# Router logits from the output projection, two token tiles a step in two PSUM banks, and one row scatter a place

## The chip, the cores and the metric

The kernel runs on one core of one Trainium2 chip, in float32. The metric is device microseconds of a whole run, the median of three runs. One further execution was recorded by the hardware profiler; every number with a line of the code beside it comes from that one.

## The reference

The input is x (4096 tokens x 256 features) and a 4096 x 4096 matrix adj. Two layers follow each other.

```python
x = x + gnn(layernorm(x), adj, neigh_W, lin_W)   # z = [f, adj @ (f @ Wn.T) / deg] @ Wl.T
x = x + ffn(layernorm(x)[None], ...)             # below; here x stands for layernorm(x)
h = rmsnorm(x, ln1)
q, k, v = heads of h @ wq.T, wk.T, wv.T          # 4 heads, 2 key/value heads, 64 wide; q, k rotated
y = softmax(causal(q @ k.T / 8)) @ v
x = x + y @ wo.T
flat = rmsnorm(x, ln2)
probs = softmax(flat @ router_w.T)               # 8 experts
tp, ti = top_k(probs, 2)                         # weights: tp / (sum + 1e-9)
out = sum over e of weight[e] * (silu(flat @ w1[e].T) * (flat @ w3[e].T)) @ w2[e].T
return x + out
```

What matters here is the stretch from y to the two chosen experts. The router's logits are a product of the normalized sum `x + y @ wo.T`. They are linear in y before the normalization, so they can be had as `y @ (wo.T @ router.T)` plus a part from x alone, and scaled afterwards.

## The kernel before, in words

The tokens are cut into 8 blocks of 512 (`NB`), each of 4 tiles of 128 (`TB`). The program has a fixed order on each engine, written out by hand; instructions of an engine run in that order, and semaphores hold them for their data.

*Stages.* (1) The graph layer, with queries, keys and values of blocks 0 to 6 made on the way (0 to 545 us). (2) Attention, blocks in the order 3, 0, 4, 1, 5, 2, 6, 7 (545 to 1072 us). (3) The experts: groups of token rows, collected by expert in the DRAM tensor `lists`, go through w1, w3 and w2 (from 1072 us).

*Attention.* A block has two head pairs; for each, a loop goes over its key tiles. One turn of it is called a unit here. A unit makes scores five units ahead (`scores`, L738: 8 matmul passes in 64x64 tiles), has ScalarE (ACT) exponentiate them (L746), adds them to running sums on VectorE (DVE, `totals`, L764), masks diagonals on GpSimd (POOL, L748) and multiplies by V (`values`, L778) into two PSUM banks. The three banks `y_first`, `y_second`, `y_third` are taken in turn, two by each pair; the pair that ends is unloaded by ACT (L786) and then DVE (L787), so one of the three is not in use by the current pair. Scores take two more double banks, and `p_ms` is a single bank for everything else.

*Places.* All other work of a block is a list of steps, and `at` (L1522) puts each list into places; a place comes after every second unit, and there are 144. A step that works on PE takes a free place; a list entry that begins with `None` doesn't ask whether the place is free. `after(b)` (L1026) is the list that follows a block's attention: `inputs` (layernormed rows), `project` twice (L850: two token tiles x two halves of y, into one `p_ms` bank, added into `row` by DVE at L859), `logits` (L888), `squared` (ACT, then a power on POOL), `residual` (L861: POOL adds, SP stores), `weigh` (L904), `choose`, `scaled`, `place` (the row's slots in the lists) and eight `scatter`s (L1004), which are indirect DMAs issued by POOL. The normalization's inverse comes before it through DRAM: `denominators`, `inverted` (SP's DMAs, L827 and L833) and `normalize` (DVE, L840).

*Logits before.* `router_wo` folds the router into wo (`router_sb`, 32 columns of which 8 are used). `logits` multiplies it with y into four 128x32 tiles (`lgT`), ACT copies that (L901), and `weigh` transposes it (`lg`, L907) and adds the part from x (`first_lg`).

*The last block.* Its queries are not ready when attention begins. `last_qkv` (L1049) makes them in the first places: `turned` (two transposes steps, `tr_l`), and four times `rotate` (`pq_l`) and `turn_heads` (`trq_l`), one token tile a step, each in `p_ms`. Its own `after` list runs among the experts: `step` (L1588) takes one entry of `rest` at fixed points of `hidden` and after `combine`.

Of the kernel before, what the change touches and what calls it, by code (L numbers as in the profile page):

```python
# [9 lines left out]
F32 = mybir.dt.float32  # L10
# [7 lines left out]
P = 128  # L18
N = 4096
C = 256  # L20
# [46 lines left out]
def fast_kernel(  # L67
# [53 lines left out]
    for e in range(NE):  # L121
        nc.gpsimd.memset(experts[:, :, e : e + 1], float(e))
    wo_sb = const.tile([P, 2, C], F32, name="wo_sb")

# [3 lines left out]
    wqkv_sb = const.tile([P, 2, 512 + NE], F32, name="wqkv_sb")  # L128
    router_sb = const.tile([P, 2, 32], F32, name="router_sb")
    nc.gpsimd.memset(router_sb, 0.0)  # L130

# [111 lines left out]
    with (  # L243
# [49 lines left out]
        def load_rest():  # L293

            w = wqkv.rearrange("(c p) o -> p c o", p=P)
            nc.sync.dma_start(wqkv_sb[:, :, 0:QK], w[:, :, 0:QK])
            nc.sync.dma_start(wqkv_sb[:, :, QK + NE :], w[:, :, QK:])
            nc.sync.dma_start(ln1_sb, ln1)
            nc.sync.dma_start(ln2_sb, ln2)

            wo_h = wo_t.rearrange("(j p d) o -> j d p o", j=2, p=2)
            for j in range(2):
                nc.sync.dma_start(wo_sb[j * HD : (j + 1) * HD], wo_h[j])
# [24 lines left out]
        def router_wo():  # L328
            transposed_wo = qT[5][:, :, 0:C]
            ps = p_pj.tile([P, 512], F32, tag="pj", name="p_wo")  # L330
            for j in range(2):
# [5 lines left out]
            nc.scalar.copy(  # L337
                router_sb[:, :, 0:NE], ps[:, 0 : 2 * NE].rearrange("p (j e) -> p j e", j=2)
            )
# [326 lines left out]
    with (  # L666
# [37 lines left out]
        def give_back(keys):  # L704
# [4 lines left out]
        p_sa = cycle((p_sc0, p_sc2))  # L709
        y_banks = cycle([  # L710
            pool.tile([P, 512], F32, tag=tag, name=name) for pool, tag, name in (
                (p_sc1, "sc", "y_first"), (p_sc1, "sc", "y_second"), (p_y, "y", "y_third"),
            )
        ])
        HP = P // 2
# [13 lines left out]
        def scores(b, p, s):  # L729
# [17 lines left out]
            if sb == b:  # L747
# [3 lines left out]
                )  # L751
            probs[b, p, s] = pt

        def totals(b, p, s):
# [13 lines left out]
        def values(b, p, s):  # L768
# [3 lines left out]
            if s == 0:  # L772
                accs[b, p] = next(y_banks), next(y_banks)
            for k in range(2):
# [74 lines left out]

        def project(b, h):  # L850
            x2 = flats[b][:, 2 * h : 2 * h + 2, 0:C]
            ps = p_ms.tile([P, 2, C], F32, tag="ms", name=f"po_{b}_{h}")
            for t in range(2):
                for c in range(2):
                    nc.tensor.matmul(  # L855
                        ps[:, t, :], ys[b, c][:, (2 * h + t) * P : (2 * h + t + 1) * P],
                        wo_sb[:, c, :], start=(c == 0), stop=(c == 1),
                    )
            nc.vector.tensor_add(x2, x2, ps)  # L859

# [26 lines left out]

        def logits(b):  # L888


            ps = p_ms.tile([P, P], F32, tag="ms", name=f"lgT_{b}")
            for c in range(2):
                for t in range(TB):
                    nc.tensor.matmul(
                        ps[32 * t : 32 * (t + 1), :], router_sb[:, c, :],
                        ys[b, c][:, t * P : (t + 1) * P],
                        start=(c == 0), stop=(c == 1), skip_group_check=True,
                        tile_position=(0, 32 * t),
                    )
            lgT = ax.tile([P, P], F32, tag="lgT", name=f"lgs_{b}", bufs=1)  # L900
            nc.scalar.copy(lgT, ps)  # L901
            picks[b] = lgT

        def weigh(b):  # L904
            ri, lgT = squares.pop(b), picks[b]
            lg = p_ms.tile([P, TB, 32], F32, tag="ms", name=f"lg_{b}")
            nc.tensor.transpose(lg.rearrange("p t e -> p (t e)"), lgT, ident)  # L907
            pr = small("r_p", b)
            nc.vector.tensor_add(pr, lg[:, :, 0:NE], first_lg[b])
# [94 lines left out]
        def scatter(b, t, k):  # L1004
            nc.gpsimd.memset(gap, 0.0)
            put = nc.gpsimd.indirect_dma_start(  # L1006
# [19 lines left out]
        def after(b):  # L1026

            return [
                [None, lambda: inputs(b)],
                [None],  # L1030
                [lambda: project(b, 0)],
                [lambda: project(b, 1)],
                [lambda: logits(b), lambda: squared(b, 0)],
                [None, lambda: squared(b, 1), lambda: residual(b)],
                [lambda: weigh(b)],
                [None],
                [None, lambda: choose(b)],
                [None, lambda: scaled(b, 0)],
                [None, lambda: scaled(b, 1)],
                [lambda: place(b), lambda: scaled(b, 2)],  # L1040
                [None, lambda: scaled(b, 3), lambda: scatter(b, 0, 0)],
                [None, lambda: scatter(b, 0, 1), lambda: scatter(b, 1, 0)],
                [None, lambda: scatter(b, 1, 1), lambda: scatter(b, 2, 0)],
                [None, lambda: scatter(b, 2, 1), lambda: scatter(b, 3, 0)],
                [None, lambda: scatter(b, 3, 1)],
            ]


        def last_qkv():  # L1049
# [15 lines left out]

            def turned(h):
                tr = p_ms.tile([P, 2, 2, P], F32, tag="ms", name=f"tr_l{h}")
                for t in range(2):
# [8 lines left out]

            def rotate(t):
                pj = p_ms.tile([P, 512], F32, tag="ms", name=f"pq_l{t}")
                room = hTs[t % 2]  # L1080
# [10 lines left out]

            def turn_heads(t):
                tr = p_ms.tile([P, 2, 2, P], F32, tag="ms", name=f"trq_l{t}")
                heads(ax, b, t, made["hT"], *made.pop(t), tr)
                if t == TB - 1:
                    for n in range(3):
                        lend(n, "late", 1)

            return [
                [None, scales], [None, norm], [lambda: turned(0)], [lambda: turned(1)],  # L1100
                [lambda: rotate(0)], [lambda: rotate(1)],
                [lambda: turn_heads(0)], [lambda: rotate(2)],
                [lambda: turn_heads(1)], [lambda: rotate(3)],
                [lambda: turn_heads(2)], [lambda: turn_heads(3)],
                *guard(),
# [413 lines left out]
        PLACES = len(keys) // 2  # L1519
        later, taken = {}, set()  # L1520

# [30 lines left out]
        for b in ORDER[:-1]:  # L1552
            end = at(max(ends[b] + 3, end - 4), after(b))
        at(end, [[None, begin_experts]])
# [12 lines left out]
        for n, (b, p, s) in enumerate(keys):  # L1567
# [13 lines left out]


        rest = [[lambda: normalize_pair(ORDER[-1], 1)]] + after(ORDER[-1]) + [
            [lambda: make_table(NB, True, NA, NW - NA)], [lambda: make_table(NB, False, NW, NG - NW)],
        ]
        rest = iter([fs for fs in ([f for f in fs if f] for fs in rest) if fs])
# [771 lines left out]
```

## Time and profile before

| what | us |
|---|---|
| runs: lowest, median, highest | 1585.32, 1586.35, 1587.05 |
| the profiled execution, whole | 1588.64 |
| its span, first to last instruction | 1586.9 |
| of which TensorE (PE) busy | 1565.8 |
| DVE, ACT, POOL busy | 1044.6, 488.4, 600.5 |
| attention, 545 to 1072: PE, DVE, ACT, POOL busy | 519.6, 413.4, 293.6, 181.4 |
| first part of the experts, 1072 to 1140: PE, DVE busy | 68.0, 27.7 |
| rest of the experts, 1140 to 1580: PE busy, of 440 | 438.5 |

The granted clock of TensorE has a mean of 0.996. In the profile, PE is TensorE's matmuls and PEld its weight loads. A float32 matmul of the program shows as two, so `po` of a step has eight lines where the code has four calls. A row of the timeline gives the start in us, the duration, the engine, the line, the operation with the tile that it writes and those that it reads, their sizes, a count of merged rows, and in brackets how long the engine stood idle before it and what ended that. The ends of matmuls are modelled; their starts are not, so times of a step are best taken from start to start.

### The profile page before, as it was taken

The page shows a single profiled execution, that of the slowest core. Times are in us where ns is not written, and L with a number is a line of the kernel's source. Part 1 is how long each engine was busy: PE and PEld are TensorE (multiplying, and loading weights), DVE is VectorE, ACT ScalarE, POOL GpSimd, SP SyncE. Part 2 cuts the span into 40 slices and gives each one's busy share as a digit, 9 for nine tenths or more (in the row PEclk, how much of TensorE's full clock was granted, in tenths as well). Part 3 has the DMA queues.
Part 4 walks back from the last instruction along what each step waited for, and adds up shares of the span by engine and source line. Part 5 has one row for each costly group of instructions (what it writes and reads, how often), then busy time and mean ns, then how long its engine had stood idle before and what let it go on. Part 6 is the DMA issues. An engine that isn't in the chain of part 4 may idle for free.

```text
span 1586.9 us, 27471 instructions
## 1 busy us (share of the span) xinstructions
PE 1565.8 (99%) x10744; PEld 1122.2 (71%) x10744; DVE 1044.6 (66%) x2090; ACT 488.4 (31%) x892; POOL 600.5 (38%) x726
## 2 busy tenths in 40 slices
PE   8999999999999999999999999999999999999997
PEld 7888888888888543344333333338899999999996
DVE  7966676677767676978887776893565444443562
ACT  1101010010010455565555545653122222222221
POOL 3446556457456341543443420412422212122213
PEclk9999999999999999999999999999999999999999
DMA  6343434443443001111111100069767777787762
GB/s 232 127 136 133 149 126 157 136 136 133 139 137 133 4 1 29 38 36 52 41 42 32 39 29 15 32 188 352 212 186 211 252 238 238 246 262 246 262 200 29
DMA packets 72602, 213.68 MB, mean 135 GB/s; under 512 B 17488, under 2 KB 49616, under 8 KB 58832
## 3 DMA queue, kind: packets, MB, share of 16 engines
q1 hardware_dynamic: 59200, 193.84, 36.0%
q0 software_dynamic: 12720, 17.47, 5.7%
q8 instruction: 86, 1.41, 0.4%
q10 hardware_dynamic: 544, 0.52, 0.1%
q14 instruction: 52, 0.43, 0.1%
HBM read 184.48 MB, written 31.47 MB: 136 GB/s over the span
## 4 chain that ended last, share of the span: by engine, by line
PE 95%; DVE 2%; ACT 1%; another core or an unknown queue 1%; DMA 1%; issue 0%; POOL 0%; SPq 0%; POOLq 0%; DVEq 0%; ACTq 0%
PE acc L496 24%; PE h L1417 20%; PE sc L738 14%; PE y_first L778 5%; PE y_second L778 5%; PE ye_y L1469 4%; PE y_third L778 4%; PE ye_y L1381 3%; PE ye_ms L1381 2%; PE pq L197 2%; PE po L855 2%; PE ph L548 2%; PE pf L467 1%; PE tx L1318 1%; PE trq L232 1%; PE tr L379 1%
## 5 line engine op out<-in xcount | busy, mean ns | idle before, releaser
L738 PE MATMUL sc<-qT_all,kT 64*64 64x512 f32 (+3 forms) x2304 | 283.1, 563 | 5.0 <-ACT res_all L746 2.0
L496 PE MATMUL acc<-a,g 128*128 128x256 f32 x1024 | 245.9, 380 | 0.0
L496 PEld LDWEIGHTS acc<-a,g 128*128 128x128 f32 x1024 | 193.0, 190 | 31.6 <-DVE vv L514 1.2
L1489 POOL DMA_INDIRECT acc_dram<-y,late x57 | 89.8, 1576 | 305.9 <-DVE y L1484 159.5
L1424 DVE TENSOR_TENSOR late<-si,h 128x256 f32<-128x256 f32 (+2 forms) x126 | 62.7, 506 | 184.2 <-ACT si L1423 179.2
L738 PEld LDWEIGHTS sc<-qT_all,kT 64*64 64x64 f32 x2304 | 80.4, 133 | 143.2 <-issue 112.1
L746 ACT ACTIVATE pt_all<-sc 128x1024 f32<-128x1024 f32 (+3 forms) x154 | 147.8, 968 | 104.8 <-PE sc L738 94.8
L1417 PE MATMUL h<-late,qT_all 128*128 128x256 f32 (+1 forms) x792 | 147.3, 345 | 0.0
L451 POOL TENSOR_TENSOR all_s<-all_s,more_sums 128x512 f32<-128x512 f32 x72 | 105.6, 1480 | 107.2 <-DVE more_sums L443 107.2
L1423 ACT ACTIVATE si<-h 128x256 f32<-128x256 f32 (+2 forms) x126 | 57.0, 453 | 278.0 <-PE h L1417 274.2
L1417 PEld LDWEIGHTS h<-late,qT_all 128*128 128x128 f32 x792 | 130.0, 191 | 14.7 <-issue 1.0
L496 PE MATMUL acc<-more_sums,g 128*128 128x256 f32 x512 | 126.3, 379 | 0.0
L764 DVE TENSOR_TENSOR late<-late,pt_all 128x1024 f32<-128x1024 f32 (+3 forms) x87 | 104.1, 1197 | 23.8 <-ACT pt_all L746 11.3
L1417 PE MATMUL h<-late,pt_all 128*128 128x128 f32 (+1 forms) x704 | 113.5, 321 | 0.0
L1417 PEld LDWEIGHTS h<-late,pt_all 128*128 128x128 f32 x704 | 103.5, 191 | 8.0
L778 PE MATMUL y_second<-pt_all,vv 64*64 64x512 f32 (+3 forms) x448 | 108.7, 559 | 0.0
L496 PEld LDWEIGHTS acc<-more_sums,g 128*128 128x128 f32 x512 | 97.2, 190 | 14.8
L778 PE MATMUL y_first<-pt_all,vv 64*64 64x512 f32 (+2 forms) x432 | 105.2, 563 | 0.4 <-issue 0.4
L1006 POOL DMA_INDIRECT lists<-row,slots x64 | 68.4, 1069 | 69.2 <-issue 69.1
L778 PE MATMUL y_third<-pt_all,vv 64*64 64x512 f32 (+3 forms) x352 | 87.1, 572 | 0.0
L381 ACT COPY qT_all<-tr 128x512 f32<-128x512 f32 x30 | 16.2, 589 | 210.5 <-PE tr L379 210.4
L1417 PE MATMUL h<-late,res_all 128*128 128x256 f32 (+1 forms) x352 | 68.3, 353 | 0.0
(349 smaller groups left out, 2982.2 us busy)
## 6 DMA issues: line engine op xcount, KB each, us to landing
a<-in_adj_dram SPq DMA_DIRECT2D x64, 1024.0 KB
qT_all<-in_w_dram SPq DMA_DIRECT2D x18, 1408.0 KB
pt_all<-in_w_dram SPq DMA_DIRECT2D x16, 1408.0 KB
res_all<-in_w_dram SPq DMA_DIRECT2D x17, 768.0 KB
pt_all<-in_w_dram SPq DMA_DIRECT2D x16, 768.0 KB
res_all<-in_w_dram SPq DMA_DIRECT2D x8, 1408.0 KB
qT_all<-in_w_dram SPq DMA_DIRECT2D x9, 768.0 KB
late<-lists SPq DMA_DIRECT2D x25, 265.0 KB
```

The costliest lines, as they stand in the source:

```text
L451: nc.gpsimd.tensor_add(all_s[:, i], all_s[:, i], sums_at[n % 2][k])
L496: nc.tensor.matmul(acc[bank][:, at, :], g[jb][:, right, k, :], m[left][:, k, :], start=(jb == 0 and k == 0 and at == 0), stop=(jb == NB - ...
L738: nc.tensor.matmul(ps[k * HP : (k + 1) * HP, j, :w], kT[sb][hd, i * P + k * HP : i * P + (k + 1) * HP], qT[b][hd, p, off:], start=True, st ...
L746: nc.scalar.activation(pt[:, :, :w], ps[:, :, :w], AF.Exp, scale=HD ** -0.5)
L764: nc.vector.tensor_add(sums[b, p][:, :, off:], before[:, :, off:], pt[:, :, : 512 - off])
L778: nc.tensor.matmul(accs[b, p][k][hd, off:], vv[sb][some, i, hd], pt[some, j, : 512 - off], start=(s == 0), stop=(s == TB * b + TB - 1),)
L1006: put = nc.gpsimd.indirect_dma_start(out=lists[:, :], out_offset=bass.IndirectOffsetOnAxis(ap=chosen[b][:, k, t, :], axis=0), in_=flats[b] ...
L1381: nc.tensor.matmul(p[number], m[left][:, j, :], m[right][:, j, :], start=(n % 4 == 0 and j == 0), stop=(j == 2), skip_group_check=True,)
L1417: nc.tensor.matmul(ps[m % 2][:, m // 2 - q, :], w13_sb[:, c, m * P : (m + 1) * P], xT[:, c, :], start=(c == 0), stop=(c == 1),)
L1424: nc.vector.tensor_mul(hT[:, q : q + both, :], si[:, 0:both, :], ps[1][:, 0:both, :])
L1469: nc.tensor.matmul(ps[h if last else 0][:, h, :], hT[:, q, cols], w2_sb[:, q, :], start=(q == 0), stop=(q == NF),)
L1489: put = nc.gpsimd.indirect_dma_start(out=(acc_dram if k < NM - LAST else out)[:, :], out_offset=at, in_=y[:, h, :], in_offset=None, comput ...
```

## The change

- `wo_sb` gets 8 more columns, which hold the folded router (`router_sb` is gone). A projection's matmul is 264 columns wide, and its last 8 are the logits' part from y. DVE adds each tile's 256 columns into `row` and its 8 columns to `first_lg`. `logits`, its ACT copy and the transpose in `weigh` are gone.
- A step works on two token tiles in two banks: `p_ms`, and the one of the three y banks that the current pair doesn't use. This holds for the projections and for `turned`, `rotate` and `turn_heads` of the last block's queries. Places at a pair's end (`taken`) are kept free of such steps.
- The first projection of a list comes one place later, `weigh` two entries after `squared` instead of one.
- For all blocks but the last, a scatter is preceded by a copy of one column of the newest exponentials (`latest`) into `gap`, where a memset was, and there is one scatter a place, at eight places (for block 6, two at four places).
- The last block has a list of its own, `after_last`: the second normalization shares a step with `inputs`, and the four projections go one tile a step in `p_ms`.

```diff
-    wo_sb = const.tile([P, 2, C], F32, name="wo_sb")
+    wo_sb = const.tile([P, 2, C + NE], F32, name="wo_sb")
...
-        y_banks = cycle([
+        y_banks = [
...
+        def two_banks(name):
+
+            return (
+                p_ms.tile([P, 512], F32, tag="ms", name=name), y_banks[y_next[0] % 3],
+            )
...
             probs[b, p, s] = pt
+            latest[:] = [pt]
...
-        def project(b, h):
-            x2 = flats[b][:, 2 * h : 2 * h + 2, 0:C]
-            ps = p_ms.tile([P, 2, C], F32, tag="ms", name=f"po_{b}_{h}")
-            for t in range(2):
+        def project(b, tiles, rooms):
+            if tiles[0] == 0:
+                picks[b] = small("r_p", b)
+            for t, ps in zip(tiles, rooms):
                 for c in range(2):
                     nc.tensor.matmul(
-                        ps[:, t, :], ys[b, c][:, (2 * h + t) * P : (2 * h + t + 1) * P],
-                        wo_sb[:, c, :], start=(c == 0), stop=(c == 1),
-                    )
-            nc.vector.tensor_add(x2, x2, ps)
+                        ps[:, 0 : C + NE], ys[b, c][:, t * P : (t + 1) * P], wo_sb[:, c, :],
+                        start=(c == 0), stop=(c == 1),
+                    )
+            for t, ps in zip(tiles, rooms):
+                x2 = flats[b][:, t, 0:C]
+                nc.vector.tensor_add(x2, x2, ps[:, 0:C])
+                nc.vector.tensor_add(picks[b][:, t, :], ps[:, C : C + NE], first_lg[b][:, t, :])
+
+        def project_two(b, h):
+            project(b, (2 * h, 2 * h + 1), two_banks(f"po_{b}_{h}"))
+
+        def project_one(b, t):
+            project(b, (t,), (p_ms.tile([P, 512], F32, tag="ms", name=f"po_{b}_{t}"),))
...
-        def logits(b):
...
         def scatter(b, t, k):
-            nc.gpsimd.memset(gap, 0.0)
+            if b == ORDER[-1]:
+                nc.gpsimd.memset(gap, 0.0)
+            else:
+                nc.gpsimd.tensor_copy(gap, latest[0][:, 0, 0:1])
...
+            at_once = 2 if b == ORDER[-2] else 1
             return [
                 [None, lambda: inputs(b)],
                 [None],
-                [lambda: project(b, 0)],
-                [lambda: project(b, 1)],
-                [lambda: logits(b), lambda: squared(b, 0)],
+                [None],
+                [lambda: project_two(b, 0)],
+                [lambda: project_two(b, 1), lambda: squared(b, 0)],
                 [None, lambda: squared(b, 1), lambda: residual(b)],
-                [lambda: weigh(b)],
                 [None],
+                [None, lambda: weigh(b)],
...
-                [None, lambda: scaled(b, 3), lambda: scatter(b, 0, 0)],
-                [None, lambda: scatter(b, 0, 1), lambda: scatter(b, 1, 0)],
...
+                [None, lambda: scaled(b, 3)],
+                *(
+                    [None, *(lambda n=n: scatter(b, n // 2, n % 2) for n in range(n, n + at_once))]
+                    for n in range(0, 2 * TB, at_once)
+                ),
+            ]
+
+        def after_last(b):
+
+            return [
+                [lambda: normalize_pair(b, 1), lambda: inputs(b)],
+                [lambda: project_one(b, 0)],
+                [lambda: project_one(b, 1)],
+                [lambda: project_one(b, 2), lambda: squared(b, 0)],
+                [lambda: project_one(b, 3)],
+                [lambda: squared(b, 1), lambda: residual(b)],
+                [lambda: weigh(b)],
...
             return [
-                [None, scales], [None, norm], [lambda: turned(0)], [lambda: turned(1)],
-                [lambda: rotate(0)], [lambda: rotate(1)],
-                [lambda: turn_heads(0)], [lambda: rotate(2)],
-                [lambda: turn_heads(1)], [lambda: rotate(3)],
-                [lambda: turn_heads(2)], [lambda: turn_heads(3)],
+                [None, scales], [None, norm],
+                [lambda: both_of(turned, "tr", 0)], [None],
+                [lambda: both_of(rotate, "pq", 0)], [None], [None],
+                [lambda: both_of(turn_heads, "trq", 0)],
+                [lambda: both_of(rotate, "pq", 1)], [None], [None],
+                [lambda: both_of(turn_heads, "trq", 1)],
                 *guard(),
             ]
...
-        later, taken = {}, set()
+        later = {}
+        taken = {n // 2 for n, (b, p, s) in enumerate(keys) if s == TB * b + TB - 1}
...
-            end = at(max(ends[b] + 3, end - 4), after(b))
+            end = at(max(ends[b] + 3, end - 8), after(b))
...
-        rest = [[lambda: normalize_pair(ORDER[-1], 1)]] + after(ORDER[-1]) + [
-            [lambda: make_table(NB, True, NA, NW - NA)], [lambda: make_table(NB, False, NW, NG - NW)],
-        ]
+        rest = after_last(ORDER[-1])
```

More of the change, by code (lines that the diff above doesn't have):

```diff
@@ L122, in fast_kernel @@
         nc.gpsimd.memset(experts[:, :, e : e + 1], float(e))
-    wo_sb = const.tile([P, 2, C], F32, name="wo_sb")
+    wo_sb = const.tile([P, 2, C + NE], F32, name="wo_sb")
     QK = 384
     wqkv_sb = const.tile([P, 2, 512 + NE], F32, name="wqkv_sb")
-    router_sb = const.tile([P, 2, 32], F32, name="router_sb")
-    nc.gpsimd.memset(router_sb, 0.0)
     cos_l = const.tile([P, TB, HD // 2], F32, name="cos_l")
@@ L302, in load_rest @@
             for j in range(2):
-                nc.sync.dma_start(wo_sb[j * HD : (j + 1) * HD], wo_h[j])
+                nc.sync.dma_start(wo_sb[j * HD : (j + 1) * HD, :, 0:C], wo_h[j])
             nc.sync.dma_start(
@@ L337, in router_wo @@
             nc.scalar.copy(
-                router_sb[:, :, 0:NE], ps[:, 0 : 2 * NE].rearrange("p (j e) -> p j e", j=2)
+                wo_sb[:, :, C:], ps[:, 0 : 2 * NE].rearrange("p (j e) -> p j e", j=2)
             )
@@ L713, in fast_kernel, with next_bank @@
             )
-        ])
+        ]
+        y_next = [0]
+        def next_bank():
+            y_next[0] += 1
+            return y_banks[(y_next[0] - 1) % 3]
+        def two_banks(name):
+            return (
+                p_ms.tile([P, 512], F32, tag="ms", name=name), y_banks[y_next[0] % 3],
+            )
+        latest = []
         HP = P // 2
@@ L772, in values @@
             if s == 0:
-                accs[b, p] = next(y_banks), next(y_banks)
+                accs[b, p] = next_bank(), next_bank()
             for k in range(2):
@@ L886, in over @@
             return v.to_broadcast([P, TB, NE])
-        def logits(b):
[L891 to L898, printed above, removed]
-                    )
-            lgT = ax.tile([P, P], F32, tag="lgT", name=f"lgs_{b}", bufs=1)
-            nc.scalar.copy(lgT, ps)
-            picks[b] = lgT
-        def weigh(b):
[L905 to L909, printed above, removed]
+        def weigh(b):
+            ri, pr = squares.pop(b), picks[b]
             nc.vector.tensor_mul(pr, pr, over(ri))
@@ L1040, in after @@
                 [lambda: place(b), lambda: scaled(b, 2)],
-                [None, lambda: scaled(b, 3), lambda: scatter(b, 0, 0)],
-                [None, lambda: scatter(b, 0, 1), lambda: scatter(b, 1, 0)],
-                [None, lambda: scatter(b, 1, 1), lambda: scatter(b, 2, 0)],
-                [None, lambda: scatter(b, 2, 1), lambda: scatter(b, 3, 0)],
-                [None, lambda: scatter(b, 3, 1)],
+                [None, lambda: scaled(b, 3)],
[3 more added lines that the diff above has]
+                ),
+            ]
+        def after_last(b):
[7 more added lines that the diff above has]
+                [lambda: weigh(b)],
+                [lambda: choose(b)],
+                [lambda: scaled(b, 0)],
+                [lambda: scaled(b, 1)],
+                [lambda: place(b), lambda: scaled(b, 2)],
+                [lambda: scaled(b, 3), lambda: scatter(b, 0, 0)],
+                [lambda: scatter(b, 0, 1), lambda: scatter(b, 1, 0)],
+                [lambda: scatter(b, 1, 1), lambda: scatter(b, 2, 0)],
+                [lambda: scatter(b, 2, 1), lambda: scatter(b, 3, 0)],
+                [lambda: scatter(b, 3, 1)],
+                [lambda: make_table(NB, True, NA, NW - NA)],
+                [lambda: make_table(NB, False, NW, NG - NW)],
             ]
@@ L1064, in norm, with turned @@
                 made["hT"] = qT[b]
-            def turned(h):
-                tr = p_ms.tile([P, 2, 2, P], F32, tag="ms", name=f"tr_l{h}")
+            def turned(h, bank):
+                tr = bank.rearrange("p (c t i) -> p c t i", c=2, t=2)
                 for t in range(2):
@@ L1076, in turned, with rotate @@
                 )
-            def rotate(t):
-                pj = p_ms.tile([P, 512], F32, tag="ms", name=f"pq_l{t}")
+            def rotate(t, pj):
                 room = hTs[t % 2]
@@ L1090, in rotate, with turn_heads @@
                 )
-            def turn_heads(t):
-                tr = p_ms.tile([P, 2, 2, P], F32, tag="ms", name=f"trq_l{t}")
+            def turn_heads(t, bank):
+                tr = bank.rearrange("p (c t i) -> p c t i", c=2, t=2)
                 heads(ax, b, t, made["hT"], *made.pop(t), tr)
@@ L1097, in turn_heads, with both_of @@
                         lend(n, "late", 1)
+            def both_of(f, name, h):
+                for k, bank in enumerate(two_banks(f"{name}_l{h}")):
+                    f(2 * h + k, bank)
             return [
-                [None, scales], [None, norm], [lambda: turned(0)], [lambda: turned(1)],
-                [lambda: rotate(0)], [lambda: rotate(1)],
-                [lambda: turn_heads(0)], [lambda: rotate(2)],
-                [lambda: turn_heads(1)], [lambda: rotate(3)],
-                [lambda: turn_heads(2)], [lambda: turn_heads(3)],
+                [None, scales], [None, norm],
[4 more added lines that the diff above has]
+                [lambda: both_of(turn_heads, "trq", 1)],
                 *guard(),
```

## The prediction

> **What bounds the kernel now.** I read the page first, then the timeline of TensorE (PE) around the removed steps, then the list of waits.
>
> ```profile
> PE 1565.8 (99%) x10744; PEld 1122.2 (71%) x10744; DVE 1044.6 (66%) x2090; ACT 488.4 (31%) x892; POOL 600.5 (38%) x726
> ...
> PE 95%; DVE 2%; ACT 1%; another core or an unknown queue 1%; DMA 1%; issue 0%; POOL 0%; SPq 0%; POOLq 0%; DVEq 0%; ACTq 0%
> ```
>
> PE is busy for 99% and holds 95% of the chain that ended last. So I count the time of each PE step, from the start of what stands before it to the start of what comes after. In attention (545 to 1072 us) the scores (`sc`) and products with V (`y_...`) run in rounds of four 64x64 tiles. A round of 512 columns starts 0.43 us after the last: 0.833 ns a column. The next view shows what an inserted step costs.
>
> ```profile
> 621.22 0.59 PE L778 MATMUL y_first<-late,vv 64*64 64x512 f32 x1
> 621.74 1.99 PE L855 MATMUL po<-wo_sb,yT 128*128 128x256 f32 x8
> 623.67 1.09 PE L738 MATMUL sc<-qT_all,kT 64*64 64x512 f32 x8
> ...
> 632.26 0.59 PE L778 MATMUL y_first<-pt_all,vv 64*64 64x512 f32 x1
> 632.78 0.64 PE L894 MATMUL lgT<-yT,router_sb 128*32 128x128 f32 x16
> 633.35 1.09 PE L738 MATMUL sc<-qT_all,kT 64*64 64x512 f32 x8
> ...
> 639.86 0.59 PE L778 MATMUL y_first<-pt_all,vv 64*64 64x512 f32 x1
> 640.38 0.33 PE L907 MATMUL lg<-ident,lgs 128*128 128x128 f32 x1
> 640.64 0.88 PE L738 MATMUL sc<-qT_all,kT 64*64 64x384 f32 x8
> ```
>
> Without the step, `sc` would start 0.43 us after the first line of each three. So `po` takes 623.67 - 621.65 = 2.02 us, of which 8 x 256 x 0.833 ns = 1.71 is streaming: 0.31 us goes to the change of shape, whatever is in the step. `lgT` takes 0.67 and `lg` 0.35. The score's first values also start 0.91 instead of 0.86 us after it, so each insertion costs 0.05 more.
>
> PE also stands still in four spots of attention. I add up each round's start less the start before it and its streaming.
>
> ```profile
> 828.48 0.70 PE L855 MATMUL po<-wo_sb,yT 128*128 128x256 f32 x2 [1.27 <-DVE yT L840]
> ...
> 878.51 0.96 POOL L1006 DMA_INDIRECT lists<-row,slots  x1 [0.19 <-issue]
> 879.48 0.11 POOL L1005 MEMSET gap<- 128x1 f32 x1
> 879.78 0.96 POOL L1006 DMA_INDIRECT lists<-row,slots  x1 [0.19 <-issue]
> ...
> 882.25 1.94 ACT L746 ACTIVATE late<-sc 128x1024 f32<-128x1024 f32 x2 [5.48 <-remote]
> ...
> 934.22 1.02 ACT L746 ACTIVATE res_all<-sc 128x1024 f32<-128x1024 f32 x1 [4.75 <-remote]
> 935.30 1.98 PE L738 MATMUL sc<-qT_all,kT 64*64 64x512 f32 x8 [1.98 <-ACT res_all L746]
> ```
>
> At 828 `po` waits for its normalized input: 2.07 us with the second half of that wait. The others come at the end of a run of row scatters: POOL issues eight of them 1.27 us apart (870.5 to 880.7, and 922.5 to 933), since only the queue's order holds them. At the end of both runs ACT has a score to exponentiate, starts it over 4 us late, and PE stops behind it. Costs: 1.55 us at 879 to 883; 2.67 at 932 to 935, and then 2.6 more, since six rounds after it start 0.85 apart, at half the clock; 0.43 at 722. Together 7.25. Why ACT waits ("remote") the trace does not say; other runs of eight (763 to 774, 1023 to 1034) have no such stop.
>
> **What the Trainium skill says.** "TensorEngine Tiling (Array Packing)", Key Properties: "Changing tiling mode (not just tile) drains the TensorE". The 0.31 us around each 128x128 step agree. "VectorE: DVE Perf Modes", The TRN2 errata, gives (N+151)/0.96 ns for an f32 two-input add: 691 for N = 512, and the trace has 680 to 690 for L859; so I estimate 424 for 256 columns (the trace has 418 for the 128x256 of L1424) and 166 for 8. "TensorE: Matmul & The Clock Gate", Part 1, halves the clock after an idle window of about 3.4 us. The trace is harder: 1.98 us idle at 935 was followed by half clock, 1.27 us at 828 was not.
>
> **The change part by part.**
>
> 1. *Logits.* In seven blocks `lgT` and `lg` go from attention: 7 x (0.67 + 0.35 + 2 x 0.05) = 7.8 us, all on PE's path. `po` gains 8 columns: 14 steps x 8 matmuls x 8 x 0.833 ns = 0.75 back. The last block has its steps among the experts, in 128x128 mode: `lgT` 0.57 (1094.92 to 1095.49) and `lg` about 0.2 go, 0.1 is added: -0.65. The ACT copy L901 (0.27 us, 8 times) and POOL's memset go too; neither is late.
> 2. *Last queries in pairs.* `tr_l`, `pq_l` and `trq_l` had 10 insertions and get 5, with the same matmuls: 5 x (0.31 + 0.05) = -1.8 us. `pq` to `trq` keeps three or four places of 3.4 us, against about 8 us of chain (two times DVE 1.1, POOL L213, L214, L217 up to 3.9, the second tile's L217 not waited for); six ACT copies (0.92 us a tile) end some 1.2 us after the step and delay only the exponential after it, which has 1.4 us to spare (3.43 us until its bank is wanted, less 1.04 for the scores and 1.03 for itself). I cost both at nothing; without that cover up to 3 us.
> 3. *One place later.* The first projection moves back by one place. The stop at 828 falls away, but the second tile now goes to `y_first`, the bank that the pair just ended leaves, whose unloading (L787) ended at 832.64, 5.70 us after that bank's last values. Two units later PE wants it at about 831.45: 1.2 us are left of 2.07. Gain 0.85, between 0 and 2.07. All other blocks project four units or more after a pair's end, later than the longest of these unloadings.
> 4. *Evacuation.* A `po` step's DVE work is 2 x (0.42 + 0.17) = 1.2 us for 0.69 before; `weigh` loses 0.18. The first bank is free after 0.6 us, as before; the second has 0.9 us more in hand. I take nothing; DVE is busy 413 of 527 us in attention, so up to 3 us of late banks belong in the range.
> 5. *Scatters one a place.* Each scatter of the six earlier blocks waits, by a copy of one column, for the newest exponential, so POOL can't run ahead: one in 3.4 us. Queued behind it on POOL are the diagonal selects, `scaled`, the power of `squared` and the residual add (with SP's store, and SP's next broadcasts behind that). A diagonal's exponential is issued after the one waited for, and its values come 5 units (8.6 us) later, so this costs nothing. Block 6 has two a place, over the same four places before the experts start. The gain is bounded by 0 and 7.25. I take 4.65, leaving out the 2.6 us at half clock: they hang on one window, and the profiled execution, 1588.64 us, lies 2.3 above the median.
> 6. *Experts' start.* Normalization and `inputs` now share a step, and the first `po` follows one group of 16 matmuls later, not two.
>
> ```profile
> 1078.62 3.35 DVE L799 RECIPROCAL rden<-rden 128x512 f32<-128x512 f32 x1 [0.76 <-ACT rden L798]
> 1082.00 0.69 DVE L800 TENSOR_TENSOR yT<-yT,rden 128x512 f32<-128x512 f32 x1
> ...
> 1084.03 1.89 PE L855 MATMUL po<-wo_sb,yT 128*128 128x256 f32 x8
> ```
>
> The 16 matmuls that start at 1077.88 end streaming at 1081.3 (16 x 256 x 0.833 ns); the input is ready at 1082.7. PE will wait: +1.45 us by the same method (0 to 2; more if the clock halves). Later steps of this list keep their numbers, and the weights' loads keep their distance, since the experts still begin at the same place.
>
> Sum: -7.8 + 0.75 - 0.65 - 1.8 - 0.85 - 4.65 + 1.45 = -13.55 us. The profiled execution (span 1586.9, 1.74 around it) would become 1575.1, or 1572.5 if its half-clock window goes too; the median of the runs, 1586.35, becomes **1572.8**.
>
> **Rivals.** *The stops have another cause.* Scatters run back to back without a stop in two runs of eight; then part 5 gives 0: -8.9, 1577.5 us. *DVE becomes the pace of the banks.* 66% busy on average, and L787 up to 5.7 us late; paired steps hold two banks, so five or six more waits like the 1.2 us at part 3: +6, 1579 us (1583 with the first rival). *The pacing makes POOL late (slower).* If the copy's wait plus one scatter (1.27 us) pushes selects beyond the 8.6 us before their values, each diagonal then waits: 64 diagonal tiles, 39% of the places hold scatters, so 25 x 1.27 = 32 us: 1572.8 + 32 = 1605 us. It decides once POOL is over 8.6 us behind; its longest other piece beside a scatter is the residual's 2.5 us, which speaks against it. *More than I count:* the half-clock window goes in every run and no new wait comes: 1568.
>
> **How the numbers follow.** Forecast 0.55 (1570 to 1576), other cause 0.22, DVE pace 0.13, still faster 0.06, POOL late 0.04. The range 1568 to 1580.5 takes the forecast, the first rival and most of the second. About 0.2% (3.2 us) is what a measurement of this kernel can tell from no change. All cases but the last, and a little of the third with the second, are faster: faster 0.93, same 0.04, slower 0.03.
>
> **What would show it.** `po` steps of about 2.07 us and no `lgT` or `lg`; five insertions in 548 to 600 us; scatters about 3.4 us apart and no ACT wait over 2 us "remote"; PE idle some 1.4 us before the first expert-stage `po` on DVE yT; a wait near 1.2 us at the project step right after a pair's end. I am wrong if the stops remain with the scatters spread, or if PE waits on DVE's additions out of the banks.

## The result, and the profile after

| | before | after |
|---|---|---|
| runs, median (lowest to highest), 4 each | 1586.66 (1585.32 to 1587.05) | 1569.67 (1568.80 to 1570.56) |
| ratio, 95% interval | | 0.9894 (0.9877 to 0.9912) |
| the profiled execution, whole | 1588.64 | 1569.29 |
| attention: first score to the experts' first `h` | 539.54 | 520.14 |
| experts: first `h` to TensorE's last matmul | 505.29 | 505.48 |

The four runs of before are the three of the table further up and one more. The kernel became 17.0 us faster in the runs' medians and 19.35 in the profiled executions. The forecast was 1572.8 us, with a range of 1568 to 1580.5. All of the gain lies in attention. The page's busy line of after (engine, us, share of the span, instructions):

```profile
PE 1548.6 (99%) x10608; PEld 1117.4 (71%) x10608; DVE 1046.2 (67%) x2130; ACT 487.0 (31%) x884; POOL 656.8 (42%) x725
```

POOL is busy for 56 us more than before. In attention the 56 copies that pace the scatters take 36.3 us where the memsets took 6.4, and the 56 scatters take 80.5 us instead of 60.6; the waits for the exponentials count as idle time. TensorE pays for this at one place (see `a_weigh`). Next the timeline of after at four places, each one that the prediction named.

```profile
671.07 1.16 PE L867 MATMUL po<-wo_sb,yT 128*128 128x264 f32 x4
672.07 1.05 PE L867 MATMUL y_first<-wo_sb,yT 128*128 128x264 f32 x4
673.05 0.88 PE L749 MATMUL sc<-qT_all,kT 64*64 64x384 f32 x8
...
721.34 0.98 POOL L1010 DMA_INDIRECT lists<-row,slots  x1 [0.41 <-issue]
726.28 0.96 POOL L1009 COPY gap<-res_all 128x1 f32<-128x1 f32 x1 [3.96 <-ACT res_all L757]
727.39 0.98 POOL L1010 DMA_INDIRECT lists<-row,slots  x1 [0.15 <-issue]
...
821.96 0.69 DVE L852 TENSOR_TENSOR yT<-yT,qT_all 128x512 f32<-128x512 f32 x1 [0.92 <-DMA qT_all<-inverses]
825.04 0.68 DVE L799 TENSOR_TENSOR yT<-yT,y_first 128x512 f32<-128x512 f32 x1
825.77 1.16 PE L867 MATMUL y_first<-wo_sb,yT 128*128 128x264 f32 x4 [0.47 <-DVE yT L799]
...
1062.32 0.69 DVE L812 TENSOR_TENSOR yT<-yT,rden 128x512 f32<-128x512 f32 x1
1063.06 0.71 PE L867 MATMUL po<-wo_sb,yT 128*128 128x264 f32 x2 [0.70 <-DVE yT L812]
```

A `po` step in two banks takes 1.98 us from its first row to the score after it; counted as in the prediction it is 2.07, as foreseen. The scatters stand 6 us apart here (two units and a projection lie between, and the copy waits for its exponential); within a block the median is 3.9 us, where 3.4 was foreseen. At 825.77 the second tile waits for the bank that the pair before has left. Its unloading (L799) stands in DVE's queue behind two multiplications, of which one waits for a DMA, and behind two of the running sums. At 1063.06 the experts' first projection waits for its normalized input. No long wait of ACT ends "remote" any more.

**How the executions are compared below.** TensorE's rows are merged, and some are missing. But all 288 exponentials of the scores on ACT (L746, in after L757) are in every trace. If I subtract the start of the n-th one in one kernel from the n-th in another, I get a curve that steps where one of them loses time. Where nothing differs it is flat to 0.01 us.

### The profile page after: what moved, and what is told of

It is laid out like the page before. It is cut to its first block, busy times and chain, and to the rows that moved or that the text cites. A ratio compares the mean times of both kernels' runs of the same rounds, so it can differ in the third digit from the quotient of the medians.

```text
span 1567.5 us, 27284 instructions
## 1 busy us (share of the span) xinstructions
PE 1548.6 (99%) x10608; PEld 1117.4 (71%) x10608; DVE 1046.2 (67%) x2130; ACT 487.0 (31%) x884; POOL 656.8 (42%) x725
## 5 line engine op out<-in xcount | busy, mean ns | idle before, releaser
L757 ACT ACTIVATE pt_all<-sc 128x1024 f32<-128x1024 f32 (+3 forms) x155 | 148.3, 962 | 104.9 <-PE sc L749 103.5
L776 DVE TENSOR_TENSOR late<-late,pt_all 128x1024 f32<-128x1024 f32 (+2 forms) x89 | 107.6, 1210 | 16.9 <-ACT pt_all L757 5.9
L790 PE MATMUL y_first<-pt_all,vv 64*64 64x512 f32 (+3 forms) x440 | 104.1, 551 | 0.0
L1010 POOL DMA_INDIRECT lists<-row,slots x64 | 88.4, 1381 | 17.7 <-issue 12.3
```

The lines of the kernel that those rows point to most:

```text
L757: nc.scalar.activation(pt[:, :, :w], ps[:, :, :w], AF.Exp, scale=HD ** -0.5)
L776: nc.vector.tensor_add(sums[b, p][:, :, off:], before[:, :, off:], pt[:, :, : 512 - off])
L790: nc.tensor.matmul(accs[b, p][k][hd, off:], vv[sb][some, i, hd], pt[some, j, : 512 - off], start=(s == 0), stop=(s == TB * b + TB - 1),)
L1010: put = nc.gpsimd.indirect_dma_start(out=lists[:, :], out_offset=bass.IndirectOffsetOnAxis(ap=chosen[b][:, k, t, :], axis=0), in_=flats[b] ...
```

## The experiments

Each is an edit of after (`a_`) or of before (`b_`). Where no kernel is named, medians are compared with after's 1569.67. Kernels that were not run side by side differ for that alone: before itself had medians from 1585.06 to 1587.55 us in four of the five sets of runs, and 1576.10 in the fifth. So the attention times of the traces, which follow the medians with "attention", say more than small differences of medians.

**Pacing alone, on before (`b_paced`).**

```diff
-            nc.gpsimd.memset(gap, 0.0)
+            nc.gpsimd.tensor_copy(gap, latest[0][:, 0, 0:1])   # but for the last block
...
-                [None, lambda: scatter(b, 0, 1), lambda: scatter(b, 1, 0)],   # two a place
+                [None, lambda: scatter(b, n // 2, n % 2)],                    # one a place, eight places
```

> Part 5 alone on the kernel before: one scatter a place behind a copy of the newest exponential, two a place for block 6. My theory: the three stops of 879 to 883, 932 to 941 and 722 us go, and no new one comes: 4.6 to 7.3 us less than before, 1579.4 to 1582 us. Rival B: no gain, 1586.7 us. Rival C (a paced scatter on GpSimd delays the diagonal selects and through them a softmax step on ScalarE, the 1.9 us stop that after has at 896 us): 2 us less of the gain, 1581.4 to 1584 us, with a TensorE wait of 1 to 2 us on ScalarE L746 in it.

Measured: 1578.19 us (5 runs; before beside them 1587.17), ratio 0.9940 (0.9926 to 0.9953): 9.0 us less. Attention fell from 539.54 to 528.52, so 11.0 us in the profiled executions. That is more than my whole upper bound of 7.25. Rival B fell; rival C's stop did not come. The curve shows why the bound was too low. At *each* row of scatters of before the exponentials come late, not only at the three that I had listed. First ACT in before at two other rows: block 3's, which I had not mentioned (last issue ending at 672.32), and block 4's, which I had called free of stops (774.38):

```profile
667.89 1.02 ACT L746 ACTIVATE late<-sc 128x1024 f32<-128x1024 f32 x1 [0.81 <-PE sc L738]
673.68 1.02 ACT L746 ACTIVATE late<-sc 128x1024 f32<-128x1024 f32 x1 [4.77 <-PE sc L738]
...
770.28 1.02 ACT L746 ACTIVATE pt_all<-sc 128x1024 f32<-128x1024 f32 x1 [2.04 <-issue]
775.42 1.94 ACT L746 ACTIVATE pt_all<-sc 128x1024 f32<-128x1024 f32 x2 [4.11 <-PE sc L738]
```

And the same exponentials with the scatters paced:

```profile
669.52 1.02 ACT L747 ACTIVATE late<-sc 128x1024 f32<-128x1024 f32 x1 [0.69 <-PE sc L739]
673.32 1.02 ACT L747 ACTIVATE pt_all<-sc 128x1024 f32<-128x1024 f32 x1 [2.78 <-PE sc L739]
...
772.62 1.02 ACT L747 ACTIVATE pt_all<-sc 128x1024 f32<-128x1024 f32 x1 [2.77 <-PE sc L739]
774.28 1.02 ACT L747 ACTIVATE pt_all<-sc 128x1024 f32<-128x1024 f32 x1 [0.64 <-PE sc L739]
```

The exponential of 673.68 is the one of 669.52: 4.2 us late. Scores run five units ahead, so most of a delay is absorbed. What stays, as steps of the curve, is 0.91 us for block 3, 0.15 each for blocks 4 and 1, 2.62 for block 5, 6.67 for block 2 (with the half clock), 1.21 for block 6. For block 0 the curve goes the other way by 0.8: the end of a row costs less there than a new stop of `b_paced`, whose next step waits 1.5 us at 722 for `p_ms`, the one bank.

**The list without the copy (`a_memset`), and part 5 undone (`a_burst`).**

```diff
-                nc.gpsimd.tensor_copy(gap, latest[0][:, 0, 0:1])
+                nc.gpsimd.memset(gap, 0.0)                 # a_memset and a_burst
...
-                [None, lambda: scatter(b, n // 2, n % 2)],
+                [None, lambda: scatter(b, 0, 1), lambda: scatter(b, 1, 0)],   # a_burst only
```

> After's lists with one scatter a place, but each scatter is again preceded by a memset instead of the copy of the newest exponential, so GpSimd may run ahead of attention. My theory (a row of scatters issued back to back stops ScalarE and then TensorE, and it is the wait for the exponential that prevents it): scatters again 1.3 us apart in rows, ScalarE waits of over 2 us that end 'remote' at the end of some rows, 4.6 to 7.3 us slower than after, 1574.3 to 1577 us. Rival A (the order of the list alone spaces the scatters, since other GpSimd work lies between them): as after, 1569.7 us. Rival B (the stops had nothing to do with scatters): 1569.7 us although the scatters stand 1.3 us apart.

Measured: 1571.49 us (4 runs), +1.8; attention +2.2. Neither side was right. The scatters stand in rows of two to eight, and most rows are shorter than in before. At four of them the exponentials come 1.5 to 2.5 us later than in after, and 0.3 to 1.5 us of each delay stays, 4.0 in all; 1.2 us less at the stop of `a_weigh` (below) and 0.7 at a bank wait stand against it. The list alone gives most of the gain.

> Part 5 of the change undone in full: memsets, two scatters a place in five places for all blocks, lists overlapping as before; the rest as after. My theory: the stops of before come back, 4.6 to 7.3 us slower than after, 1574.3 to 1577 us. Rival B (the stops of before came from where its logits and projections stood, not from the scatters): 1569.7 us, as after.

Measured: 1580.90 us (5 runs), +11.2; attention 531.57, +11.4. The stops are back with after's own projections and logits around them, so rival B fell. ACT and TensorE at the end of block 5's row, with the last of POOL's issues:

```profile
872.53 0.96 POOL L1007 DMA_INDIRECT lists<-row,slots  x1 [0.19 <-issue]
...
874.97 1.02 ACT L757 ACTIVATE late<-sc 128x1024 f32<-128x1024 f32 x1 [5.48 <-remote]
...
876.05 1.98 PE L749 MATMUL sc<-qT_all,kT 64*64 64x512 f32 x8 [2.94 <-ACT late L757]
```

ACT starts again 1.48 us after the last issue has ended (872.53 + 0.96). In before it was 1.36, 1.04, 1.51 and 1.27 for blocks 3, 4, 5 and 2. For block 0 ACT started 0.48 us before the last issue had ended, and block 6 had no wait of over 2 us.

What ACT waits for can be read from the times at which semaphores are incremented, which the traces hold too. The last matmul of a score increments the semaphore that the score's exponential waits for:

| kernel and row | that matmul ends (modelled) | increment recorded | ACT starts |
|---|---|---|---|
| before, block 3 | 669.42 | 673.66 | 673.68 |
| before, block 4 | 771.60 | 775.40 | 775.42 |
| before, block 5 | 876.27 | 882.23 | 882.25 |
| before, block 2 | 929.03 | 934.20 | 934.22 |
| `a_burst`, block 5 | 869.20 | 874.95 | 874.97 |
| `b_paced`, the same exponential as before's of 882.25 | 875.79 | 875.84 | 875.86 |

With the scatters paced the increment follows the matmul by 0.05 us. At the rows it comes 3.8 to 6.0 us late, and ACT starts 0.02 us after it. So at these rows TensorE's work was done in time, and its *signal* was late. A second increment follows each of the five late ones by 0.16 us, so two scores were waiting to be announced. The first increments of the row's last scatter stand within 0.3 us of the late ones (673.62, 775.69, 882.05, 934.26 and 874.80). Why the signals are late the traces don't say. The record of increments is not complete there: the last scatters of blocks 3, 4 and 2 have 16 each, most others in a row three to five.

**More scatters, thin scatters, or only a busy POOL (`a_wide8`, `a_thin8`, `a_pool10`).** The first two send the rows once more to a tensor that nobody reads; `a_thin8` sends four columns only. The third multiplies rows by one. All come ahead of the paced scatters, for seven blocks.

```diff
+        def burst(b):
+            for n in range(2 * TB):                                  # a_wide8, a_thin8
+                nc.gpsimd.memset(gap, 0.0)
+                nc.gpsimd.indirect_dma_start(out=spare[:, :], ...,   # slots as in scatter
+                    in_=flats[b][:, n // 2, :], in_offset=None)      # a_thin8: 0:4
+            for n in range(10):                                      # a_pool10
+                x2 = flats[b][:, n % TB, 0:C]
+                nc.gpsimd.tensor_scalar(x2, x2, 1.0, None, op0=ALU.mult)
```

> After, and on top of it, for each block but the last, just before its paced scatters, eight more row scatters back to back (1060 bytes a row, 128 rows each) into a DRAM tensor that nobody reads. Theory D (a row of indirect DMAs issued back to back stops ScalarE and TensorE): stops of 0.5 to 7 us at the ends of the new rows, 9 to 11 us in all as between the kernel with bursts and after, 1579 to 1581 us. Theory P (the time that GpSimd is occupied is what counts): the same. Rival (the stops come from the scatters that the later program waits for, not from their being issued): 1569.7 us.

Measured: 1602.10 us (4 runs), +32.4; attention +34.1. That is three times what I expected; the rival fell.

> The same eight more scatters a block, but 16 bytes a row instead of 1060. If the number of descriptors or of instructions on GpSimd stops the other engines: as with wide rows, 1579 to 1581 us. If the bytes moved do (0.95 MB a run against 0.014): 1569.7 to 1571 us.

Measured: 1613.91 us (4 runs), +44.2; attention +42.5. Neither number was right, but thin rows do stop the other engines. Part of the loss in both kernels is at half clock: TensorE's mean granted clock is 0.992 and 0.987 in the two profiled executions, 0.999 in after's. (A row of eight moves 8 x 128 x 1060 bytes = 1.09 MB wide and 0.016 thin; the expectation has these a little too low.)

> After, and at the same place of each block but the last ten GpSimd multiplications of a 128x256 tile by one (about 1 us each, back to back), with no DMA in them: GpSimd is occupied for as long as with eight scatters. Theory P (occupied GpSimd is late with the diagonal selects[...], and so the others wait): stops as with the scatters, 1579 to 1581 us. Theory D (it is the issue of DMAs): 1569.7 to 1571 us.

Measured: 1570.46 us (4 runs), +0.8; attention +2.3, of which 1.5 is the bank wait of 825.77, grown to 1.97. POOL and ACT in `a_thin8`, block 0's row:

```profile
720.39 1.37 POOL L1027 DMA_INDIRECT spare<-row,slots  x1 [0.19 <-issue]
722.06 1.03 POOL L1027 DMA_INDIRECT spare<-row,slots  x1 [0.19 <-issue]
...
715.46 1.02 ACT L757 ACTIVATE pt_all<-sc 128x1024 f32<-128x1024 f32 x1 [0.57 <-PE sc L749]
724.92 0.58 ACT L826 COPY dens<-dn 128x512 f32<-128x512 f32 x1 [8.44 <-remote]
```

And the same stretch in `a_pool10`:

```profile
711.62 7.31 POOL L1025 TENSOR_SCALAR row<-row 128x256 f32<-128x256 f32 x7
...
717.38 0.59 ACT L826 COPY dens<-dn 128x512 f32<-128x512 f32 x1 [1.60 <-PE dn L821]
```

ACT stands idle for 8.44 us beside DMAs; beside multiplications that fill POOL as well it is 1.60. TensorE's matmuls for the sum to be copied end at 717.34 and 717.32; the increment is recorded 7.6 us later beside DMAs (724.90) and 0.04 us later beside multiplications (717.36). So a busy POOL is not the cause, nor are the bytes: thin rows are worse than wide ones. What is left is the indirect DMAs themselves, one close behind another. Whether it is their issue on POOL, or their packets and the increments at their ends, no run separates. An issue takes the same time thin and wide (medians 1026 and 1022 ns). That agrees with the Trainium skill, "DMA: Bandwidth & Descriptors", SWDGE vs HWDGE vs iDMA: software on GpSimd computes the descriptors and appends them to rings, so an issue's length should go with the descriptors and not with the bytes. The page says nothing of other engines being held up.

**Logits undone (`a_logits`).**

```diff
-                        ps[:, 0 : C + NE], ..., wo_sb[:, c, :],
+                        ps[:, 0:C], ..., wo_sb[:, c, :],
...
-                nc.vector.tensor_add(picks[b][:, t, :], ps[:, C : C + NE], first_lg[b][:, t, :])
...
-                [None, lambda: squared(b, 1), lambda: residual(b)],
+                [lambda: logits(b), lambda: squared(b, 1), lambda: residual(b)],
```

> Part 1 of the change undone, the rest as after: the projection 256 columns wide again, the logits' own 128x32 step (in the place of the second squaring), its ScalarE copy and the transpose in the weighing. My sum: 7 x (0.67 + 0.35 + 0.1) - 0.75 + 0.65 = 7.7 us more than after, 1577.4 us. Counted by the traces of before and after, per block 1.05 less 0.1 for the projections, and 0.65: 7.3 us. Rival (the two steps filled TensorE time that waits would have taken anyway): under 3 us more, below 1572.7 us.

Measured: 1577.50 us (5 runs), +7.8; attention +7.24, experts +0.79. In the curve the two steps are +0.63 and +0.42 in each block (at the 56th and 60th exponential, and again at the 248th and 252nd). The rival fell.

**Queries undone (`a_single`).**

```diff
-                [lambda: both_of(rotate, "pq", 0)], [None], [None],
+                [lambda: one_of(rotate, "pq", 0)], [lambda: one_of(rotate, "pq", 1)],   # and so on
```

> Part 2 undone, the rest as after: the last block's queries one token tile a step, ten insertions in the single bank instead of five in two. My sum: 5 x 0.36 = 1.8 us more, 1571.5 us; counting 0.31 alone, 1.55 us more. Rival (the pairs' ScalarE copies and rotation chains delay the scores, so single steps cost nothing): 1569.7 us or less, with TensorE waits on ScalarE in 545 to 600 us of after that single steps lack.

Measured: 1572.04 us (5 runs), +2.4. The curve has +1.53 by the end of the queries, which is 5 x 0.31, and then nothing until the bank wait of block 5 (+3.0 with half clock after it). The edit doesn't touch that wait, and it differs from trace to trace: by the prediction's method it is 0.63 us in after, 1.20 in `a_norm` and 1.95 here, and the instructions around it are the same. The rival fell.

**The normalization in a step of its own (`a_norm`).**

```diff
-                [lambda: normalize_pair(b, 1), lambda: inputs(b)],
+                [lambda: normalize_pair(b, 1)], [lambda: inputs(b)],
...
-                [lambda: project_one(b, 3)], [lambda: squared(b, 1), lambda: residual(b)],
+                [lambda: project_one(b, 3), lambda: squared(b, 1), lambda: residual(b)],
```

> Part 6 undone, the rest as after: the last block's second normalization has a step of its own ahead of its inputs, so the first projection among the experts comes two groups of 16 matmuls after the denominators (the fourth projection shares the step of the second squaring, so that all later steps keep their numbers). The 0.87 us that TensorE waits there in after (1063.06, on VectorE yT) should go: 1568.8 us. Rival (a wait moves to another step, as the fourth projection stands close to the squaring): 1569.7 us.

Measured: 1569.20 us (4 runs), -0.5, too little for runs that were not made side by side; the experts' stretch is 504.51 instead of 505.48, so the edit gives 0.97. Attention is 0.58 longer, which is block 5's bank wait again.

**The weighing one place earlier (`a_weigh`).**

```diff
-                [None],
                 [None, lambda: weigh(b)],
+                [None],
                 [None, lambda: choose(b)],
```

> After with the router's weighing one place earlier, two places ahead of its exponential as in the kernel before, not one. After has a stop of 1.9 us at 895.5 to 897.5: ScalarE waits 2.46 us with the router's exponential for VectorE's maximum, which stands in VectorE's queue behind sums that wait for diagonal selects behind GpSimd's residual and scatters; the scores' exponentials stand behind it. My theory: with one more place between them the stop goes, 1.9 us less than after, 1567.8 us. Rival (the select is as late for the score sums, so TensorE stops anyway a little later): as after, 1569.7 us.

Measured: 1568.68 us (4 runs), -1.0, ratio to before 0.9879 (0.9864 to 0.9894). The stop in after:

```profile
893.11 1.53 POOL L1010 DMA_INDIRECT lists<-row,slots  x1 [0.18 <-issue]
894.66 0.42 POOL L759 TENSOR_SCALAR_AFFINE_SELECT pt_all<-pt_all 128x256 f32<-128x256 f32 x1
895.12 0.43 DVE L776 TENSOR_TENSOR late<-late,pt_all 128x256 f32<-128x256 f32 x1 [1.43 <-POOL pt_all L759]
895.68 0.19 DVE L913 TENSOR_REDUCE r_top<-r_p 128x4 f32<-128x32 f32 x1
896.33 0.23 ACT L920 ACTIVATE r_p<-r_p 128x32 f32<-128x32 f32 x1 [2.46 <-DVE r_top L913]
896.47 1.01 ACT L757 ACTIVATE qT_all<-sc 128x1024 f32<-128x1024 f32 x1
897.53 0.66 PE L749 MATMUL sc<-qT_all,kT 64*64 64x512 f32 x4 [1.73 <-ACT qT_all L757]
```

Read from above: a paced scatter delays a diagonal select, that a sum on DVE, behind which the router's maximum stands, for which ACT's small exponential waits, and behind it the exponential that TensorE needs. Four queues, each in order. With the weighing earlier the curve drops by 1.73 us at that unit, and is 0.9 up at block 5's bank wait. Without the pacing the stop is gone as well: the curves of `a_burst` and `a_memset` drop by 1.73 and 1.17 at the same unit. And `b_paced`, which has the pacing but weighs two places ahead, lacks the stop. So it takes both parts of the change.

**All repairs (`a_best`, then `a_three`).** `a_best` put the third repair on block 1; the bank wait is block 5's.

```diff
-                [None], [None], [lambda: project_two(b, 0)],
+                *([[None]] * (3 if b == 5 else 2)), [lambda: project_two(b, 0)],   # a_three; a_best: block 1
```

> After with three repairs: the router's weighing one place earlier (1.0 us less in its own run), the normalization in a step of its own (0.87), and block 1's two projections one place later, so that their second tile no longer asks for the bank that the pair before has just left (0.7 us in after, 1.5 with the weighing moved). If the three are independent: 1.0 + 0.87 + 0.7 to 1.5 = 2.6 to 3.4 us less than after, 1566.3 to 1567.1 us. Rival (the bank is late there too, or the denominators' exchange is): no less than the first two give, 1567.8 us.

Measured: 1569.61 us (4 runs): no gain over after. The two other repairs hold (-1.73 in the curve, experts 504.51), but block 5's wait was 1.90 us in the profiled execution, and the clock was half for four rounds after it (they start 0.82 to 0.91 us apart instead of 0.43): +3.1.

> The three repairs again, the third now on the right block: the step whose second tile waits for the bank of the pair before is block 5's (two units after a pair's start), not block 1's. Block 5 projects one place later (four units after the pair's start), its choice comes one place later too, and its last scaling shares the first scatter's place, so that its list keeps its length; for all blocks the weighing is one place earlier, and the last block's second normalization has its own step. If the three stops go (0.63 to 2.1 us, 1.73, 0.97) and none comes: attention 518 us from its first score to the experts' first step instead of 520.1, and 1566 to 1567 us. Rival (VectorE's queue, whose head waits for the broadcast of the inverses, is late for the other places too): a wait on yT of about 1 us remains at block 5's projection, 1567.5 us or more.

Measured: 1565.95 us (5 runs), the lowest of all medians. Attention 517.63 and experts 504.51: 3.5 us less than after, with all three stops gone. Block 5's projections:

```profile
828.04 1.16 PE L867 MATMUL po<-wo_sb,yT 128*128 128x264 f32 x4
829.03 1.05 PE L867 MATMUL y_first<-wo_sb,yT 128*128 128x264 f32 x4
830.02 0.88 PE L749 MATMUL sc<-qT_all,kT 64*64 64x384 f32 x8
```

The second tile starts without a wait. But beside these runs before itself took 1576.10 us (9 runs, 1575.79 to 1577.82), nine to eleven less than beside all others. The ratio to it is 0.9934 (0.9920 to 0.9947). These runs were made on another chip (number 14) than the other experiments (7, 9 and 13), and after was not run there, so the two medians don't show what the repairs gain; the traces do. The loss of before is thus no constant of the program. That those ten are the scatters' stops fits in size, but there is no trace of before from that chip.

## Why the prediction was right, step by step

| step of the sum | forecast | measured | from |
|---|---|---|---|
| 1 logits, attention | -7.05 | -7.24 | `a_logits` |
| 1 logits, last block | -0.65 | -0.79 | `a_logits` |
| 2 queries in pairs | -1.8 | -1.53 | `a_single`, curve |
| 3 first projection | -0.85 | -0.9 | curve from `b_paced` to after at block 5, less 1.03 for its logits |
| 4 evacuation | 0 | 0 | no wait of `po` on L873 or L874 in after |
| 5 scatters | -4.65 | -11.0 on before, -11.4 within after (the next row's stop counted in) | `b_paced`, `a_burst` |
| 5 POOL's delay of others | 0 | +1.7 | `a_weigh`, curve |
| 6 experts' start | +1.45 | +0.97 | `a_norm` |

With part 5 as measured on before the terms sum to -18.8 (-7.24 - 0.79 - 1.53 - 0.9 - 11.0 + 1.7 + 0.97), with part 5 as measured within after to -20.9. The profiled executions differ by 19.35, between the two; the edits are not quite independent, and `a_burst` has a bank wait that is 0.8 us longer.

The forecast came nearer than its largest term, and that was partly luck. Part 5 gained 6.4 us more than the sum has. Against it stand a stop that I had not foreseen (1.7), and the profiled executions, which differ by 2.4 us more than the medians. Without these two the median would have been about 1566 us (my estimate: 1569.67 - 1.7 - 2.4), below the range. The measured 1569.67 lies just under the 1570 to 1576 to which I gave 0.55, nearest to "more than I count", which had 0.06; and the new waits that this case leaves out did come.

- **Right in kind and size:** 1 and 2. An insertion costs its streaming and 0.31; the 0.05 more that I charged doesn't show in the pairs.
- **Right in kind, and in size partly by chance: 3.** I foresaw the exchange of a wait for `yT` with a wait for a bank, at this step, with 1.2 us. The bank wait is 0.6 to 2.1 us in eight traces, of which after's 0.63 is the shortest, and absent in three (`a_memset`, `a_wide8`, `a_thin8`); the unloading stands behind an instruction that waits for a DMA. The two waits differ by 2.07 - 0.63 = 1.4, and the curve has only 0.9 of it.
- **Right in kind, wrong in size: 5.** The term to blame is "together 7.25", cut to 4.65. I listed TensorE's stops row by row, and wrote that "other runs of eight (763 to 774, 1023 to 1034) have no such stop". ACT's 4.77 and 4.11 us of idle time at 673.68 and 775.42 stood in the trace of before, labelled "PE sc" instead of "remote", and I passed over them: by the curve the rows that I left out cost 2.4 us (0.91, 0.15, 0.15 and 1.21). The rows that I had listed cost more than TensorE's stops there show: 2.62 us for 1.55 at block 5, and 6.67 for 5.27 at block 2. Leaving out the half clock was wrong too.
- **Not foreseen:** that "this costs nothing" fails where a chain of small steps crosses the queues. I had costed the delay against the diagonals' own deadline of 8.6 us, not against the weighing, which the change also moved next to its exponential. The rival of a late POOL came true at one place.
- **Too high: 6.** 1.45 took all of `po` to wait for the normalized half. Its first matmuls read the other head pair, and TensorE lost 0.87.

The reason given for part 5, that POOL issues eight in a row, stands, and rows of other POOL work don't do it. What holds ACT meanwhile is the late increment of a semaphore: the exponential of 882.25 waits for TensorE alone, whose matmuls for it ended at 876.27, and the increment is recorded at 882.23. What holds the increment back stays open.

## What to carry to other kernels

Spread GpSimd's indirect DMAs among other work; a row of eight back to back held up engines that did not wait for it, and cost TensorE 0.15 to 6.7 us in before. Look for such losses in the idle times of *all* engines around the event, whatever the releaser is called, hold the end of the work that an engine waits for against the increment of its semaphore, and compare two traces by an instruction that occurs once per unit. When a queue is delayed on purpose, follow the smallest instruction behind it through every further queue.

## What the runs showed of the hardware

- Indirect DMAs of 128 rows, issued 1.3 to 1.6 us apart from GpSimd, cost 0.61 us each of TensorE's time with 1060 bytes a row (34.1 us for 56) and 0.76 with 16 bytes (42.5), half clock included. At four rows of before and one of `a_burst` ACT resumes 1.0 to 1.5 us after the last issue has ended.
- At these rows the increment of TensorE's semaphore is recorded 3.8 to 6.0 us after the matmul that makes it, in `a_thin8` 7.6 us; beside multiplications on GpSimd (`a_pool10`) 0.04 us, with paced scatters (`b_paced`) 0.05.
- TensorE's clock was halved after an idle time of 1.78 us (`a_single`, at 828.62) and 1.90 (`a_best`, at 827.29), but not after 1.97 at the same step (`a_pool10`): the granted clock just after them is 0.50 in the first two and 1.00 in the third. The Trainium skill, "TensorE: Matmul & The Clock Gate", Part 1, speaks of a window of about 3.4 us; these waits are shorter, and their length alone doesn't decide.
